# Seven quarter products for the source part of a four-layer adjacency aggregation

## Chip, cores, metric

One core of one Trainium2 chip. The time is the device time of one execution in microseconds (us), median of several runs; lower is better. All timed runs used here of one kernel agreed within 0.6%.

## The reference, cut to what matters

Sixteen independent batches, each with 1024 nodes of 128 features and a dense 1024x1024 adjacency, all fp32. Layer 0 aggregates once with the raw adjacency. Then come four message layers with 1, 1, 2 and 3 chunks of 128 input features, which use the adjacency with normed rows (source part) and with normed columns (destination part):

```python
def _layer(nodes, adj, ws, bs, wd, bd, wn, bn, wu, bu):
    src_agg = jnp.einsum('bjv,bij->biv', nodes @ ws + bs, _l2norm(adj, 2))
    dst_agg = jnp.einsum('bjv,bji->biv', nodes @ wd + bd, _l2norm(adj, 1))
    self_rep = nodes @ wn + bn
    return jnp.tanh(jnp.concatenate([src_agg, self_rep, dst_agg], axis=2) @ wu + bu)
# layers three and four concatenate features kept from earlier layers
x = _layernorm(x + _L0_gnn_ref(x, adj, adj, W, b))        # layer 0
x = _layernorm(x + _L1_gnn_ref(x, adj, ...))              # layers one to four
```

## The kernel before

The adjacency is held twice: as loaded with columns scaled (`a`, destination part) and transposed with rows scaled (`at`, source part). Messages are computed first (`messages`), then `aggregate` runs pairs of products of 64 columns side by side, one into partitions 64 to 127 (`high`) and one into 0 to 63 (`low`) of PSUM banks. The destination part is a 2x2 block product done by seven quarter products instead of eight (Strassen's scheme in Winograd's form), from sums of quarters `T2`, `T3`, `T4` of the adjacency and sums `S` of the messages. The source part is direct: eight blocks for each half of the nodes and each half of the features.

```python
upper = [                                    # into partitions 64..127
    (pz0, True, own(1, 0) + [src(1, 0, j) for j in range(4)], None),
    (alpha, True, dst(0, 0, quarter(a, 0, 0)), first_read),
    (pz0, False, [src(1, 0, j) for j in range(4, NB)], None),
    (alpha, True, mixed(2, T2), second_read),
    (pz0, False, dst(1, 1, T4), None),
    (alpha, True, mixed(3, T3), third_read),
    (pz1, True, own(1, 1) + [src(1, 1, j) for j in range(2, NB)], None),
]
lower = [                                    # into partitions 0..63
    (pz0, True, own(0, 0) + [src(0, 0, j) for j in range(NB)], None),
    (pz1, True, mixed(1, T1) + [src(1, 1, j) for j in range(2)], fourth_read),
    ...                                      # (cut)
]
for i, pair in enumerate(zip(up, lo)):
    if i in hooks:
        hooks[i]()        # work of other engines, and small products, ahead of pair i
    for o, x, y, start, stop, _ in pair:
        nc.tensor.matmul(o, x, y, start=start, stop=stop)
```

In the traces read here TensorE, VectorE and ScalarE run their instructions in the order of the program: in layer three `rp`, with key 5, comes behind 20 records of pairs (four a pair). So a key in `hooks` is a place in TensorE's order. While a batch runs its layers, the next batch's adjacency is loaded, its rows summed and squared (`sums`: ScalarE squares, GpSimd adds them up), its columns' sums of squares taken (`column_sums`, then a product `pc`), scaled, and its layer 0 is computed between layers three and four. Two small products: `rp` spreads the inverse norms of rows (layer three), `pv` sums squares for a layer norm (in layer four for the next batch, in layer one for the batch before).

```python
hooks = {0: factors, 5: factors_of_rows, 10: ...}              # layer three; rp is in factors_of_rows
hooks = {0: squares0, 5: rstd0, 11: end0, 15: rows0, ...}      # layer four; pv is in rstd0
hooks = {12: centre1, 18: rstd1, 27: end1}                     # layer one; pv is in rstd1
```

## Time and profile before

| | before |
|---|---|
| time, median | 2648.96 us |
| span in the profile | 2647.7 us |
| TensorE busy / not busy | 2592.4 / 55.3 us |
| mean granted TensorE clock (share of full speed) | 0.993 |

"Not busy" is the span less the busy time; it is the sum of all waits of TensorE, with start and end. Which waits those are is told by the view of waits (engine, tile, line, releaser: us in total, times, longest; PE is TensorE, PEld its loading of weights, DVE VectorE, ACT ScalarE, POOL GpSimd, SP SyncE, which issues transfers, and a q behind a name is that engine's queue):

```profile
PE pa L612 <- DMA raw<-in_L_gnn_wd_dram: 12.3, 1, 12.3
PE pv L325 <- DVE v L319: 7.6, 18, 2.2
...
PE rp L261 <- DVE sp L257: 2.4, 1, 2.4
```

A count of 1 is the start of the program. In the steady part only `pv` waits, some 0.25 to 0.4 us each time: TensorE is the bound.

### The profile page before, as it was taken

To read this page: it belongs to the slowest core of one execution; us is meant where nothing else is said; L and a number is where in the kernel's file an instruction comes from. 1 tells how busy PE (TensorE), PEld (TensorE's weight loads), DVE (VectorE), ACT (ScalarE), POOL (GpSimd) and SP (SyncE) were. 2 spreads that over 40 slices of the span, in tenths; PEclk is the share of its full clock that TensorE was granted. 3 is DMA by queue.
4 is the path that set the end of the run, shared out by engine and by line. 5 is a ranking of instruction groups with operands and counts; after the bars stand their busy time and mean duration, and the time that the engine had idled before them with its cause. 6 is when DMAs were issued, how large, how long until landed. Compare 5 with 4: busy or idle time off the path is not lost.

```text
span 2647.7 us, 29748 instructions
## 1 busy us (share of the span) xinstructions
PE 2592.4 (98%) x11313; PEld 1111.6 (42%) x11313; DVE 1517.7 (57%) x1978; ACT 731.2 (28%) x1374; POOL 505.5 (19%) x217
## 2 busy tenths in 40 slices
PE   5999999999999999999999999999999999999997
PEld 3444443433444344443444434334443444434443
DVE  5746656465564746557366564655647465574622
ACT  4413223141322413224132231413224132241311
POOL 5301203022030210303012030210302103030100
PEclk8999999999999999999999999999999999999998
DMA  7515214251241614315252142512315143152100
GB/s 163 107 49 113 48 57 92 58 125 45 71 77 51 125 45 102 64 53 105 58 114 48 57 92 58 126 45 75 73 50 126 45 104 63 55 103 58 50 9 8
DMA packets 358927, 196.44 MB, mean 74 GB/s; under 512 B 158800, under 2 KB 337872, under 8 KB 358784
## 3 DMA queue, kind: packets, MB, share of 16 engines
q1 hardware_dynamic: 355728, 190.27, 32.1%
q0 software_dynamic: 1648, 3.87, 0.7%
q8 instruction: 89, 1.46, 0.2%
q10 hardware_dynamic: 1408, 0.40, 0.1%
q14 instruction: 54, 0.44, 0.1%
HBM read 177.41 MB, written 17.02 MB: 73 GB/s over the span
## 4 chain that ended last, share of the span: by engine, by line
PE 94%; DVE 4%; DMA 1%; POOL 0%; SPq 0%; issue 0%; POOLq 0%; ACT 0%; ACTq 0%; DVEq 0%
PE p L527 67%; PE pt L423 15%; PE pa L350 8%; PE pw L361 1%; PE pw L362 1%; DVE v L319 1%; DVE y L310 1%; DMA raw<-in_L_gnn_bu_dram 1%; PE pv L325 0%; DVE t L427 0%; DVE at L386 0%; PE pm L309 0%; DVE t L436 0%; DVE S L437 0%; DMA raw<-in_L_gnn_wn_dram 0%
## 5 line engine op out<-in xcount | busy, mean ns | idle before, releaser
L527 PE MATMUL p<-at,t 128*64 128x512 f32 x3840 | 1133.7, 594 | 2.1 <-DVE at L386 2.1
L527 PE MATMUL p<-a,t 128*64 128x512 f32 x1536 | 687.1, 593 | 0.0
L527 PEld LDWEIGHTS p<-at,t 128*64 128x64 f32 x3840 | 356.6, 137 | 489.1 <-issue 477.9
L329 POOL TENSOR_TENSOR rs<-ve,mhalf 128x32 f32<-128x32 f32 (+1 forms) x34 | 174.4, 5130 | 1682.5 <-DVE ve L327 1682.5
L527 PE MATMUL p<-T,S 128*64 128x512 f32 x1024 | 463.5, 593 | 0.0
L427 DVE TENSOR_TENSOR t<-pt,bsd 128x512 f32<-128x512 f32 x256 | 173.9, 684 | 200.3 <-PE pt L423 200.3
L527 PEld LDWEIGHTS p<-a,t 128*64 128x64 f32 x1536 | 207.9, 137 | 147.3 <-issue 146.5
L527 PEld LDWEIGHTS p<-T,S 128*64 128x64 f32 x1024 | 139.0, 137 | 281.7 <-issue 279.6
L216 POOL TENSOR_TENSOR acc<-acc,sq 128x1024 f32<-128x1024 f32 x90 | 214.8, 2387 | 124.6 <-ACT sq L212 121.0
L527 PE MATMUL p<-T,t 128*64 128x512 f32 x512 | 233.4, 594 | 0.0
L527 PE MATMUL p<-a,S 128*64 128x512 f32 x512 | 233.2, 593 | 0.0
L381 ACT ACTIVATE st<-st,rinv 128x256 f32<-128x256 f32 x512 | 210.6, 494 | 14.5 <-DMA st<-in_adj_dram 12.0
L423 PE MATMUL pt<-wall,f1T 128*128 128x256 f32 x768 | 213.5, 383 | 0.0
L287 DVE TENSOR_TENSOR a<-a,cinv 128x1024 f32<-128x1024 f32 (+1 forms) x132 | 146.4, 1172 | 113.1 <-DMA cinv<-dr 105.2
L350 PE MATMUL pa<-a,xn 128*128 128x512 f32 x480 | 210.0, 595 | 0.0
L386 DVE STREAM_TRANSPOSE at<-st 128x512 f32<-128x512 f32 x256 | 162.0, 682 | 7.3 <-issue 7.3
L471 ACT COPY e<-p 64x512 f32<-64x512 f32 x64 | 37.2, 581 | 453.3 <-PE p L527 453.3
L423 PEld LDWEIGHTS pt<-wall,f1T 128*128 128x128 f32 x768 | 142.8, 190 | 44.7 <-issue 26.1
L527 PE MATMUL p<-f1T,wall 128*64 128x512 f32 x384 | 149.0, 601 | 0.0
L480 ACT COPY e<-e 64x512 f32<-64x512 f32 x64 | 39.3, 615 | 366.8 <-DVE e L479 366.8
L350 PEld LDWEIGHTS pa<-a,xn 128*128 128x128 f32 x480 | 90.0, 190 | 119.8 <-issue 119.8
L210 DVE TENSOR_REDUCE cols<-a 128x1 f32<-128x1024 f32 x120 | 139.0, 1208 | 0.5
(138 smaller groups left out, 2817.0 us busy)
## 6 DMA issues: line engine op xcount, KB each, us to landing
st<-in_adj_dram SPq DMA_DIRECT2D x1024, 64.0 KB, 2.0
a<-in_adj_dram SPq DMA_DIRECT2D x120, 512.0 KB, 12.8
xn<-in_x_dram SPq DMA_DIRECT2D x128, 64.0 KB, 1.9
kept<-y SPq DMA_DIRECT2D x16, 512.0 KB, 2.8
xk<-kept SPq DMA_DIRECT2D x16, 512.0 KB, 3.8
xs<-in_x_dram SPq DMA_DIRECT2D x60, 128.0 KB, 13.4
cinv<-dr SPq DMA_DIRECT2D x30, 256.0 KB, 6.3
dinv<-dr SPq DMA_DIRECT2D x30, 256.0 KB, 5.2
```

Source lines behind the costliest of these rows:

```text
L210: nc.vector.reduce_sum(cols[:, 2 * NB + i:2 * NB + i + 1], a[:, i, :], axis=AX.X)
L216: nc.gpsimd.tensor_add(acc, acc, sq)
L287: engine.tensor_mul(a[:, i, s], a[:, i, s], cinv[:, s])
L329: nc.gpsimd.tensor_tensor(rstd, ve, mhalf[:, :n], ALU.pow)
L350: nc.tensor.matmul(pa, xn[:, i], a[:, i, s], start=(i == 0), stop=(i == NB - 1))
L381: nc.scalar.activation(st[:, k], st[:, k], AF.Copy, scale=rinv[:, q * QB + k:q * QB + k + 1])
L386: nc.vector.transpose(at[h][:, j:j + NJ, o:o + QB * C].rearrange("p j (k c) -> p j k c", c=C), st.rearrange("p k (j c) -> p j k c", c=C)[: ...
L423: nc.tensor.matmul(pt[:, q], f[:, i * P:(i + 1) * P], w[:, c, 0:2].rearrange("p k v -> p (k v)"), start=(k == 0), stop=(k == nch - 1))
L427: nc.vector.tensor_add(t[j][:, o:o + 2], pt, bsd[l][:, None, :].to_broadcast([P, 2, 2 * P]))
L471: nc.scalar.copy(e0[high], alpha[high])
L480: nc.scalar.copy(e1[high], e0[high])
L527: nc.tensor.matmul(o, x, y, start=start, stop=stop)
```

## The change

The intent: use seven quarter products for the source part too, in layers two to four, and pay for the room it needs (three sums of quarters `Q2`, `Q3`, `Q4` of the transposed side) by staging rows in the old adjacency's place, fetching message weights again from memory for each layer, and sharing other buffers. The second half of the nodes is finished first. The heart of the diff, for layers two to four, with cuts:

```diff
-        upper = [ (pz0, True, own(1, 0) + [src(1, 0, j) ...]), (alpha, True, dst(...)), ... ]
+            upper = [
+                (Z1, True, own(1, 1)), (Z0, True, own(1, 0)),
+                (A, True, prod("M1", DST) + prod("M1", SRC)), (Bk, True, prod("M2", DST) + prod("M2", SRC)),
+                (A, True, prod("M3", SRC)),
+                (Z0, False, prod("Z21", SRC) + prod("Z21", DST)),
+            ]
+            lower = [
+                (Z1, True, own(0, 1)), (Z0, True, own(0, 0)),
+                (A, True, prod("M4", DST) + prod("M4", SRC)), (Bk, True, prod("M3", DST)),
+                (Z1, False, prod("Z12", SRC) + prod("Z12", DST)),
+                (Z0, False, prod("Z11", SRC) + prod("Z11", DST)),
+            ]
+            events = {8: first_reads, 12: lambda: nc.scalar.copy(e1[high], Bk[low]), 16: m2_and_half_of_m3,
+                      20: last_reads}
@@ sums
-            nc.vector.reduce_sum(cols[...], a[:, i, :], axis=AX.X)
+            if i < BPH:
+                nc.scalar.activation(sq, a[:, i, :], AF.Copy, accum_out=degree)
+            else:
+                nc.vector.reduce_sum(degree, a[:, i, :], axis=AX.X)
@@ layer one
-            hooks = {12: centre1, 18: rstd1, 27: end1}
+            hooks = {0: begin1, 10: centre1, 12: squares1, 14: rstd1, 20: end1}
@@ layer two
+            for i in ((3, 4) if b == 0 else (2, 3, 4)):
+                combine(i, yt, Q)                      # Q2, Q3, Q4 at step 0
+            for i in ALL:
+                hooks[1 + 3 * i] = lambda i=i: sums(n, a2, st, (i,))
+            hooks[26] = lambda: column_sums(n, st)
+        aggregate(b, 1, feats, t, a, at, T, Q, f23, "acc", hooks)
@@ layer three
-            hooks = {0: factors, 5: factors_of_rows, 10: lambda: scale(0), ...}
+            hooks = {1: factors, 11: lambda: scale(0, 1), ...}     # factors now holds rp too
@@ layer four
-            hooks = {0: squares0, 5: rstd0, 11: end0, 15: rows0, 19: rows1, 23: rows2, "half": rows3, 33: rows4}
+            hooks = {0: squares0, 3: rstd0, 10: rows0, 11: end0, 18: quarters0, 23: rows1, 26: rows2, 31: rows3}
```

Note for later that `Bk` is one bank with two users: the lower half takes `M3`, which ScalarE copies out at step 12 (counted without the own products), and the upper half takes `M2`, whose products go on from step 12.

## The prediction

> **What bounds the kernel now.** I read, in order, the page's busy times and slices, the chain of waits that ended last, the timeline of VectorE and TensorE at the starts of layers, and the groups by line.
>
> ```profile
> PE 2592.4 (98%) x11313; PEld 1111.6 (42%) x11313; DVE 1517.7 (57%) x1978; ACT 731.2 (28%) x1374; POOL 505.5 (19%) x217
> ...
> PE   5999999999999999999999999999999999999997
> ```
>
> TensorE is busy in all slices but the first and last; VectorE is busy little more than half of the time. Busy time alone does not prove a bound, so the chain is next (start us, length us, what), one piece of one batch:
>
> ```profile
> 1272.77 4.44 PE p L527 x20
> 1277.21 0.34 PE rp L261 x2
> 1277.55 25.04 PE p L527 x116
> 1302.60 13.93 PE pa L350 x32
> ...
> 1319.96 10.37 PE pt L423 x48
> 1330.33 0.02 issue
> 1330.36 0.69 DVE t L427
> 1331.05 1.13 DVE y L310
> ...
> 1333.96 1.14 DVE v L319
> 1335.10 0.04 issue
> 1335.15 0.41 PE pv L325 x2
> 1335.56 26.76 PE p L527 x124
> ```
>
> The chain lies on TensorE except for about 5 us at the start of layer four, where it runs over VectorE. There TensorE was still mostly working: its wait for pv was about 0.4 us. The unit to count in: one step of the aggregation is a pair of 64-column products, run beside each other, and leaves four records (two products, two passes each). So 116 records are 29 pairs in 25.04 us: 0.863 us a pair. A batch holds 134 pairs (115.7 us), the message stages (3.65, 3.65, 7.11 and 10.37 us in the chain, 24.8 together), 16 pa products (13.9), 4 pw (3.4) and six small products of about 0.34 us (2.0): 159.8 us. The same point of the next batch in the trace is 160.66 us later. So TensorE does nothing but work: each pair removed is worth 0.863 us, and each new wait of TensorE costs its full length.
>
> [...] So a small product that waits for VectorE holds everything behind it; the 0.4 us wait for pv above agrees. [...] 128x512 takes 0.69 us and 128x2048 2.29 us. Back to back they start 0.61 us apart for 128x512. [...] in layer two, beside the row sums on GpSimd (line L216), the small 128x256 combinations took 2.47 us instead of 0.42:
>
> ```profile
> 1239.34 2.47 DVE L436 TENSOR_TENSOR t<-t,t 128x256 f32<-128x256 f32 x1
> 1241.85 2.46 DVE L437 TENSOR_TENSOR S<-t 128x256 f32<-128x256 f32 x1
> 1244.23 0.28 DVE L439 TENSOR_TENSOR diff<-t 128x128 f32<-128x128 f32 x1
> ```
>
> **The change, part by part.**
>
> *Pairs.* Counting the two lists of the aggregation: 2n+30 pairs in each layer before (n = chunks of features). After: layer one still 2n+30, layers two to four 2n+28. Only two pairs fewer, because seven quarter products instead of eight save the source part one of eight, which is 4 of its 32 half-width products. That is 3 x 16 x 2 = 96 pairs, 96 x 0.863 = 83 us, all on the bound. This is the whole gain: an ideal 2566 us.
>
> *VectorE.* Four quarter sums of 128x2048 on the transposed side are added per batch: 4 x 2.29 = 9.2 us. Four row reductions of 1.21 us go to ScalarE (-4.8). The message combinations grow from 128x256 to 128x512 in layers two to four, about +1.2 us each. Some +8 us a batch; VectorE goes from 57% to some 62%. On average nothing, so what matters is where TensorE waits for it.
>
> *Order at the start of a layer.* Two things come together: the four combinations, which VectorE does in order ahead of everything else, take longer; and the small products that depend on later VectorE work are placed earlier in TensorE's order. I followed the order of instructions in the built changed kernel with durations from these lines:
>
> ```profile
> 1272.81 0.69 DVE L427 TENSOR_TENSOR t<-pt,bsd 128x512 f32<-128x512 f32 x1 [1.04 <-PE pt L423]
> 1273.42 0.42 DVE L435 TENSOR_TENSOR S<-t 128x256 f32<-128x256 f32 x1
> ...
> 1275.78 0.15 DVE L257 TENSOR_TENSOR sp<-inv,group 128x32 f32<-128x32 f32 x1
> ...
> 1277.14 0.41 PE L261 MATMUL rp<-sp,fold 128*128 128x32 f32 x2
> ```
>
> Layer three (messages end at 1272.7 here). Before, rp comes after five pairs and sp was done at 1275.9: no wait. After, rp comes after one pair, at 1273.6. VectorE: message add at 1272.8, combinations at +0.6, +1.3, +2.0, +2.7, the first factor instruction at +3.4, the end of sp 0.7 later: 1276.9. TensorE waits 3.3 us. 15 batches have a successor: 50 us.
>
> Layer four. pv comes after three pairs instead of five: pm ends at 1330.4, so TensorE is there at 1333.0. VectorE: add 1330.4, centring 1331.0, four combinations from 1332.1 with 0.6 to 0.7 us each, the reduction v (1.21 us) from 1334.8 to 1336.0. Wait 3.0 us, less the 0.4 of before: 2.6 x 15 = 39 us.
>
> Layer one (15 batches). The distance from pm to pv was six pairs and is four, 3.45 us. Between them VectorE now does a part of e0 (0.6), the centring (1.2), a quarter sum T4 (2.2) that has been put ahead of v, and v (1.2): 5.2 us. Wait about 1.4 us: 21 us.
>
> Layer two. The first quarter products need the sum of messages, right after two own pairs (1.7 us); VectorE needs about 2.0 us: 0.3 us x 16. At its end the column sums wait for GpSimd's last addition, which starts later than before because the next adjacency is loaded later; I get the second half of the features up to 1 us late: 0.6 x 15. Together 14 us.
>
> *Transfers.* Rows go straight from the old adjacency's place; before, 137 GB/s came at half the DMA engines' share. 1 MB should take 5 to 8 us and is then scaled and transposed some 20 us later: hidden. The next adjacency is loaded some 17 us later in layer one and takes 20 us at 206 GB/s; its first half lands just as ScalarE wants it. Refetched weights (at most 512 KB) are hidden by a whole layer.
>
> *Start and end.* Batch 0 multiplies columns before its first quarter product, where eight source pairs used to hide it: about +5 us. The first weights no longer fetch ahead of the adjacency: a few us either way. The tail stays the same.
>
> *Sum.* 2649 - 83 + 50 + 39 + 21 + 14 + 5 = 2695 us.
>
> **Rivals.** (A) The waits are hidden and the pairs count in full: 2566 to 2590 us, faster. For it: TensorE is the bound in every slice, and the change's intent. Against: the two long waits follow from in-order engines and durations that the trace shows, and before had just 0.4 us to spare at one of the very places. (B) The waits grow: GpSimd's additions hold the quarter sums in layer two (0.42 us became 2.47), or the idle of 3 us drops the granted clock. In the start of this trace an idle of about 3 us near 62 us was followed by a clock of 0.5 for some 3 us, one of 2 us near 88 us was not. One such drop costs at most 1.7 us; in every batch at two places 50 us. 2720 to 2750 us, slower. (C) A late transfer (rows or adjacency) holds ScalarE, which is in order, and then the features: 2 to 3 us a batch, 2725 to 2745.
>
> **Range and chances.** The mechanism puts the waits at 7 us a batch at least, against 5.2 saved, so about 2670 is the low side; hidden additions of (B) and (C) push up more often than down. Range 2655 to 2740. The border of slower is 2702, only 7 us above my number. Faster 0.05, within 2% 0.57, slower 0.38.
>
> **What would show it.** Right: some 384 aggregation records fewer on TensorE (96 pairs of four); a batch of about 163.5 us; waits of TensorE for sp (about 3 us, 15 times), for v in layer four (about 3) and in layer one (about 1.4), with the chain going over VectorE's combinations there. Wrong: a batch of 155 to 156 us with rp and pv not waiting (A); a clock clearly under 0.99, or VectorE additions of over 4 us beside GpSimd (B); waits for DMA on ScalarE or TensorE in the steady part (C).

The sum (2695 us): its durations are those of the trace of the kernel before (the 0.69 and 2.29 us are fp32 additions on VectorE). That the work behind a waiting product waits too, the runs show at `rp`: in the changed kernel the products behind it stood still for its 3.40 us, and where seven more pairs were put ahead of it they ran and the wait was gone (e2_rp). The 1.7 us of a drop of the clock are an estimate from the same trace: after the idle time near 62 us (3.00 us) the clock was 0.50 for some 3.4 us.

## The result

Ratios here are the mean time of one kernel's runs over that of the kernel before in the same rounds, so not quite the ratio of the medians quoted.

The changed kernel takes **2908.75 us** (4 runs, 2907.93 to 2911.35), ratio 1.0983 (95%: 1.0964 to 1.1002). It is 260 us slower; the prediction was 46 us slower. First the page of the changed kernel: the busy times, and the chain that ended last by engine ("issue" is time in which an engine waited for nothing that the profile shows).

```profile
PE 2611.0 (90%) x10929; PEld 1145.0 (39%) x10929; DVE 1674.3 (58%) x1974; ACT 830.0 (29%) x1549; POOL 511.9 (18%) x217
...
PE 64%; DVE 13%; DMA 8%; SPq 5%; ACT 4%; issue 4%; POOL 2%; POOLq 0%; DVEq 0%; ACTq 0%
```

The same line of the chain for the kernel before:

```profile
PE 94%; DVE 4%; DMA 1%; POOL 0%; SPq 0%; issue 0%; POOLq 0%; ACT 0%; ACTq 0%; DVEq 0%
```

TensorE has 384 records fewer, as intended, and only 64% of the chain lies on it (94% before). Yet its busy time *rose*, by 18.6 us, where the removed 96 pairs should have lowered it by 82.8. That contradiction is worth stopping at: fewer records that take longer in all must be slower records. The mean granted clock says the same: 0.966 against 0.993. So the difference of the two spans, 258.1 us, splits exactly:

- work removed: 96 x 0.863 = -82.8 us
- TensorE not busy: 294.8 (2905.8 - 2611.0) against 55.3: **+239.5 us**
- the rest of the busy time, 2611.0 - (2592.4 - 82.8) = **+101.4 us**. I call it stretch. Counted in slices of 3 us between 150 us and 60 us before the end, the changed kernel has 35 separate drops of the clock, 143 us at half speed in all, the kernel before none; so about 72 us of the stretch are seen directly there. Over the whole span the mean clock accounts for at most some 80 us of it (about 98 us of clock lost, 18 before); the other 20 or so are not explained.

The view of waits names the 239.5:

```profile
PE pv L347 <- DVE v L341: 73.4, 32, 3.0
PE p L581 <- ACT e L559: 69.8, 48, 3.6
PE rp L283 <- DVE sp L279: 51.5, 16, 3.4
PE pt L445 <- DVE t L448: 31.1, 15, 3.0
PE p L581 <- ACT e L502: 20.1, 16, 1.3
```

Three places show how these come about. **Layer three**, the chain of waits (start, length, what), just after the last message group:

```profile
1402.03 0.70 DVE S L458
...
1403.48 0.70 DVE S L460
...
1404.21 0.69 DVE S L461
...
1405.46 0.08 DVE sp L279
...
1405.68 0.60 PE rp L283 x2
```

VectorE works through four combinations before it comes to `sp`, and `rp` stands one pair behind the messages in TensorE's order: a wait of 3.4 us. Layer four has the same picture with `pv` behind v (3.0 us). Both are as predicted.

**Layer two** is what the prediction did not have. ScalarE's timeline, then TensorE's (start, length, engine, line, operation, shape; in brackets the idle time before and its releaser):

```profile
1374.31 1.06 ACT L231 ACTIVATE sq<-a 128x1024 f32<-128x1024 f32 x1
...
1375.49 1.06 ACT L234 ACTIVATE sq<-a 128x1024 f32<-128x1024 f32 x1
...
1376.55 1.04 ACT L234 ACTIVATE sq<-a 128x1024 f32<-128x1024 f32 x1
...
1377.70 0.58 ACT L559 COPY e<-p 64x512 f32<-64x512 f32 x1
```

```profile
1371.26 3.76 PE L581 MATMUL p<-T,S 128*64 128x512 f32 x15
1378.33 1.12 PE L581 MATMUL p<-Q,S 128*64 128x512 f32 x1 [3.32 <-ACT e L559]
...
1381.76 0.59 PE L581 MATMUL p<-Q,S 128*64 128x512 f32 x1
```

L559 is the copy of `Bk[low]`. The next product of `M2` goes to `Bk[high]`, other partitions of the same bank, and it waits for that copy. TensorE's last products end at 1375.0. The copy could run then, but ScalarE, in order, has one pass over 1024 columns under way and two more ahead of it, and runs it at 1377.70. The wait is in the program: the built code has, on the first product on `Q`, a wait for ScalarE. It could have been read before predicting; I took reads and writes of different partitions to be independent. The built program here waits for the whole bank (or for the tile, which fills the bank; the two can't be told apart here), at up to 3.6 us a time, though the copy reads partitions 0 to 63 and the products write 64 to 127. Whether they could run side by side here no run shows: taking the wait away alone was not tried.

**The clock.** The same lines show the second cost: the product after the wait takes 1.12 us, and 0.59 us three microseconds later. The windows view (window, length, busy us and count of each engine, then granted clock, DMA share, GB/s):

```profile
1379.00:1382.00 3.00, 3.00 (x10) 0.85 (x8) 0.00 (x0) 1.15 (x2) 2.84 (x3) 0.55 0.00 0
1382.00:1386.00 4.00, 4.00 (x20) 1.26 (x18) 1.54 (x3) 1.51 (x2) 2.00 (x1) 1.00 0.00 0
```

In the first window 0.55 is the clock: TensorE counts as busy for the whole 3 us and does little more than half the work. In the batch from 1343 to 1520 us this happens three times, after the waits of 3.32 (L559), 3.40 (rp) and 3.04 us (pv); not after those of 1.6 us and below. In these three the granted clock is 0.50 to 0.55 and a drop lasts some 3.4 us. The whole run is less regular. Laid beside the records of the clock, its 35 drops (28 of some 3.4 us, 7 of some 6.8) follow all 15 waits of `rp` (3.40 us), but only 8 of the 15 waits of `pv` in layer four (3.04 us), 10 of the 14 in layer two (2.88 to 3.58 us), and 2 waits of `pt` (1.74 and 2.73 us); none follows the 15 waits of `pv` in layer one (1.60 us). So the length of a wait alone does not decide whether a drop follows.

### The profile page after: what moved, and what is told of

The parts are those of the page before. It is cut to its first block, busy times and chain, and to the rows that moved or that the text cites. A ratio compares the mean times of both kernels' runs of the same rounds, so it can differ in the third digit from the quotient of the medians. Undisturbed runs are those within 1.5% of the kernel's fastest.

```text
span 2905.8 us, 28577 instructions
## 1 busy us (share of the span) xinstructions
PE 2611.0 (90%) x10929; PEld 1145.0 (39%) x10929; DVE 1674.3 (58%) x1974; ACT 830.0 (29%) x1549; POOL 511.9 (18%) x217
## 4 chain that ended last, share of the span: by engine, by line
PE 64%; DVE 13%; DMA 8%; SPq 5%; ACT 4%; issue 4%; POOL 2%; POOLq 0%; DVEq 0%; ACTq 0%
PE p L581 43%; PE pt L445 11%; PE pa L372 7%; DMA a<-in_adj_dram 5%; SPq L217 2%; POOL rs L351 2%; SPq L396 2%; DVE at L406 2%; DVE t L448 2%; DVE y L332 1%; DVE v L341 1%; ACT a L401 1%; DMA out_dram<-y 1%; PE pw L383 1%; PE pw L384 1%
## 5 line engine op out<-in xcount | busy, mean ns | idle before, releaser
L581 PE MATMUL p<-at,t 128*64 128x512 f32 x2112 | 583.4, 593 | 0.0
L581 PE MATMUL p<-a,t 128*64 128x512 f32 x1536 | 481.2, 602 | 6.1 <-DVE a L425 5.5
L581 PE MATMUL p<-Q,S 128*64 128x512 f32 x768 | 359.7, 624 | 69.8 <-ACT e L559 69.8
L581 PE MATMUL p<-T,S 128*64 128x512 f32 x1024 | 301.3, 594 | 20.1 <-ACT e L502 20.1
L581 PEld LDWEIGHTS p<-at,t 128*64 128x64 f32 x2112 | 195.9, 137 | 213.2 <-issue 192.7
L448 DVE TENSOR_TENSOR t<-pt,wm 128x512 f32<-128x512 f32 x256 | 173.0, 686 | 157.5 <-PE pt L445 156.8
L581 PE MATMUL p<-at,S 128*64 128x512 f32 x448 | 224.9, 646 | 0.0
L445 PE MATMUL pt<-wm,f1T 128*128 128x256 f32 x768 | 214.8, 385 | 0.0
L401 ACT ACTIVATE a<-a,rinv 128x256 f32<-128x256 f32 x480 | 197.3, 493 | 23.0 <-DMA a<-in_adj_dram 22.9
L581 PE MATMUL p<-Q,t 128*64 128x512 f32 x384 | 172.6, 592 | 0.0
```

The source lines that it names most:

```text
L401: nc.scalar.activation(st[:, k], st[:, k], AF.Copy, scale=rinv[:, q * QB + k:q * QB + k + 1])
L445: nc.tensor.matmul(pt[:, q], f[:, i * P:(i + 1) * P], wm[:, 1 + c], start=(k == 0), stop=(k == nch - 1))
L448: nc.vector.tensor_add(t[j][:, o:o + 2].rearrange("p k a v c -> p k (a v c)"), pt, wm[:, 0][:, None, :].to_broadcast([P, 2, 2 * P]))
```

## The experiments

All kernels gave the right result. Edits are on the changed kernel unless said otherwise. Idle is the span less TensorE's busy time; stretch is busy time above the work at full clock, as worked out above (2509.6 us, for e4 38.8 more, for e8 and before 2592.4, so that before has none by definition). Both are from one profiled run each; median and ratio from the timed runs.

| run | median us | ratio to before | clock | idle | stretch |
|---|---|---|---|---|---|
| before | 2649 | 1 | 0.993 | 55.3 | 0 |
| changed | 2908.75 | 1.0983 | 0.966 | 294.8 | 101.4 |
| e1_bank | 2947.76 | 1.1118 | 0.940 | 277.2 | 166.2 |
| e2_rp | 2830.16 | 1.0678 | 0.973 | 236.6 | 81.0 |
| e3_pv4 | 2828.27 | 1.0674 | 0.975 | 241.4 | 76.0 |
| e4_fill | 2887.73 | 1.0897 | 0.968 | 249.7 | 91.8 |
| e5_shift | 2734.41 | 1.0313 | 0.978 | 165.8 | 52.2 |
| e6_shift_bank | 2684.13 | 1.0124 | 0.981 | 122.6 | 48.3 |
| e7_quarters_early | 2678.52 | 1.0101 | 0.978 | 119.8 | 57.1 |
| e8_before_early | 2724.94 | 1.0276 | 0.989 | 116.4 | 13.9 |
| e9_place | 2659.41 | 1.0039 | 0.982 | 102.8 | 42.0 |
| e10_place_quarters | 2659.11 | 1.0032 | 0.983 | 101.5 | 41.6 |
| e11_reduce | 2620.36 | 0.9886 | 0.991 | 88.2 | 24.1 |
| e12_last_sum | 2590.21 | 0.9775 | 0.991 | 63.7 | 14.0 |

My theory: the removed pairs are worth what they should be, and placement loses more than that; each named wait is a separate cost, and waits of 3 us cost more than their length. The main rival: the waits stand for one another, because VectorE, ScalarE and GpSimd finish the same chain at the same time wherever TensorE waits for it; take one away and the next shows.

**e1_bank**: the copies out of the shared bank wait until both halves are done.

```diff
-            events = {4: m1_read, 6: lambda: m4_read(Bk), 8: m2_read, 12: m3_read, 18: second_half}
+            events = {4: m1_read, 8: m4_and_m2_read, 12: m3_read, 18: second_half}
@@ layers two to four
             def m2_and_half_of_m3():
+                nc.scalar.copy(e1[high], Bk[low])
                 m2_read()
-            events = {8: first_reads, 12: lambda: nc.scalar.copy(e1[high], Bk[low]), 16: ..., 20: last_reads}
+            events = {8: first_reads, 16: ..., 20: last_reads}
```

> The changed kernel with one thing moved: the ScalarE copies out of the lower half of the accumulator bank that M2 is still filling in its upper half are issued only after M2 is done (in layer one beside the second read, in layers two to four at step 16 instead of 12). Theory (same-bank wait): M2 or its second half waits for that copy, which in layer two stands behind the row sums in ScalarE's order; the waits for lines L559 and L502 (about 110 us of weight-load waits plus 34, some 6 to 7 us a batch with the copy itself) go, and with the 3.3 us one in layer two goes a drop of the clock (1.7 us). Expected 90 to 130 us off 2909: 2780 to 2820. Rival (VectorE is behind as a whole, so a wait removed comes back at the next small product): under 40 us off, above 2870, with longer waits for v and sp.

Measured: 39 us *slower* than the changed kernel, a plain miss. Waits of TensorE:

```profile
PE pv L347 <- DVE v L341: 90.4, 32, 3.0
PE rp L283 <- DVE sp L279: 52.0, 16, 3.4
PE pt L445 <- DVE t L448: 45.4, 15, 4.2
PE pc L264 <- DVE part L246: 40.9, 16, 5.0
```

The waits for L559 and L502 (89.9 us) are gone; pv grew by 17.0, pt by 14.3, and pc, which did not wait in the changed kernel after the start (5.0 us), has 40.9 with it. Idle fell by 17.6 us only, and stretch rose by 64.8. The trace shows why: the wait of pv in layer one went from 1.60 to 2.73 us, pt's from 1.59 to 2.92 or 3.68, and pc's from nothing to 2.39 us, and each of these was followed by a drop of the clock. In slices of 3 us there are 74 drops instead of 35. So the rival holds here, with an addition: breaking waits of 3.3 us into several of 2.4 to 3 us cost more clock here than it saved waiting.

**e2_rp** and **e3_pv4**: one small product each, later in TensorE's order.

```diff
-            hooks = {1: factors, 11: lambda: scale(0, 1), ...}
+            hooks = {1: factors, 8: factors_of_rows, 11: lambda: scale(0, 1), ...}   # e2: rp
-            hooks = {0: squares0, 3: rstd0, 10: rows0, ...}
+            hooks = {0: squares0, 8: rstd0, 10: rows0, ...}                            # e3: pv of layer four
```

> The changed kernel with only the product rp of layer three moved from behind pair 1 to behind pair 8. Theory of the prediction (the wait for sp costs its length): 3.4 us times 15 off, 51 us; with the clock drop that follows it (about 1.6 us, granted clock 0.5 for some 3.4 us) 75 us: 2830 to 2860. If the clock drop does not belong to this wait: 2855 to 2860. Rival (VectorE behind as a whole): under 20 us off.

> The changed kernel with only the product pv of layer four moved from behind pair 3 to behind pair 8. Theory: the wait of 3.0 us and the clock drop after it (1.6 us) go, 45 to 70 us off: 2840 to 2865. The norm then ends later on VectorE, some 4 us, which may give 0 to 15 us back through the transposes at the end of the layer. Rival: under 20 us off.

Measured: -79 and -80 us, a little more than expected for each. By the table e2 takes 58.2 us from idle and 20.4 from stretch, e3 53.4 and 25.4. In e2 the wait for sp is gone; in e3 pv's falls from 73.4 to 27.7, so layer four's share was 45.7 us, 3.0 a batch. These two waits are separate costs, and each microsecond of idle time that goes takes another 0.35 to 0.48 of stretch with it. In e2 that is a net figure: the 15 drops after rp are gone, while the waits of pv in layer four are now followed by a drop in all 15 batches instead of 8.

**e4_fill**: the first pair of layer three is computed three times more before rp, 45 useless pairs.

```diff
+            again = 3 if l == 2 and i == 0 and b + 1 < B else 0
-            for o, x, y, start, stop in pair:
+            for o, x, y, start, stop in [p[:4] + (True,) for p in pair] * again + list(pair):
```

> The changed kernel with useless work added: in layer three the first pair is computed three more times (2.6 us of TensorE, same result since each starts afresh) just ahead of rp, where TensorE waits 3.4 us for sp. Theory [...]: the clock stays at 1 after rp, so although TensorE does 45 pairs more the kernel gets faster, by about 1.6 us times 15, 15 to 25 us: 2884 to 2894, and the mean granted clock rises from 0.966 to about 0.975. Rival (the clock drop comes from something else, or its cost is not on the path): the time stays within 5 us of 2909 or gets longer.

Measured: -21 us, with 38.8 us more work. This is within the expectation, but not all of it for the expected reason: the wait for sp fell by 37.7 us, which the work replaces; pt's wait fell by 7.3, and stretch by only 9.6. Counted over the whole trace, the 15 drops after rp are gone, but pv's waits in layer four are followed by 15 drops instead of 8, and the time at half speed falls only from 143 to 137 us. Doing useless work cost nothing here against waiting; that the clock by itself is worth 15 to 25 us at this place is not shown.

**e5_shift**: rp and pv of layer four as in e2 and e3, pv of layer one from step 14 to 18 with its end later, and the scaling of one chunk of rows in layer four from 26 to 24.

```diff
-            hooks = {0: begin1, 10: centre1, 12: squares1, 14: rstd1, 20: end1}
+            hooks = {0: begin1, 10: centre1, 12: squares1, 14: rows1_1, 18: rstd1, 20: combine1, 26: end1}
-            hooks = {0: squares0, 3: rstd0, ..., 23: rows1, 26: rows2, 31: rows3}
+            hooks = {0: squares0, 8: rstd0, ..., 23: rows1, 24: rows2_scale, 26: rows2, 31: rows3}
```

> The changed kernel with the small products moved back behind work that does not wait: rp of layer three behind pair 8, pv of layer four behind pair 8, pv of layer one behind pair 18 (the row transposes stay at 14), and the scaling of row chunk 3 on ScalarE two steps earlier in layer four. The waits for the bank copies (L559, L502) stay. If the waits add up: 79 us (e2) plus 81 us (e3) plus about 3 us times 15 for layer one plus 1.6 times 15 for the late message sums: 2909 - 79 - 81 - 45 - 24, about 2680. If they come back elsewhere, as they did in e1: 2720 to 2800. Moving only makes the changed kernel as fast as before (2649) at best, since the bank waits stay.

Measured: 2734.41, in the range for waits that come back elsewhere. All waits of rp, pv and pt are gone from the steady part. What is left:

```profile
PE p L581 <- ACT e L559: 92.2, 48, 5.6
PE p L581 <- ACT e L502: 20.1, 16, 1.3
```

L559 grew from 69.8 to 92.2: again a part of what was removed came back at the next place. Pv of layer one and the chunk of rows were moved together, so neither is measured by itself.

**e6_shift_bank** puts e1's edit on e5.

> The one before, and also the bank copies moved behind both halves (as in e1). Theory from e1 (layer two is bound by another chain: ScalarE squares, GpSimd additions, column sums, pc): the waits for L559 and L502 go, but in layer two a wait for the column sums of about 2.4 us and a clock drop remain; about 2 us a batch off against the one before at most: 2640 to 2680. If the bank waits were what bounds layer two: 6 us a batch off, 2580 to 2600.

Measured: 2684.13, 50 us below e5, more than the 2 us a batch expected at most, and just above the expected range. The same edit that cost 39 us alone gains 50 here, which fits that fewer other waits stand ready. In the place of the 112 us for L559 and L502 stand pc (41.0) and the messages of layer three, which wait 31.4 us for the features of layer two.

**e7_quarters_early**: on e6, the sums Q2 and Q3 move from the start of layer two to the end of layer one, to unload VectorE where the chain now lies.

```diff
-            hooks = {..., 20: combine1, 26: end1}
+            hooks = {..., 20: combine1, 22: lambda: quarters1(2), 24: lambda: quarters1(3), 27: end1}
-            for i in ((3, 4) if b == 0 else (2, 3, 4)):
+            for i in ((3, 4) if b == 0 else (4,)):
```

> The one before, and two of the three quarter sums of the transposed side moved from the start of layer two to the end of layer one, where VectorE is idle for 5 us and GpSimd runs nothing. Theory (in layer two the quarter sums and GpSimd's additions hold each other up: Q3 took 4.34 us instead of 2.29): the additions end some 3 to 5 us earlier, the wait for the column sums goes, and with it its clock drop: 30 to 60 us off against the one before, 2580 to 2630, faster than the kernel before. Rival (the chain is bound by ScalarE's copies and squares alone, or by the late load): under 10 us off.

Measured: 2678.52, a miss: VectorE's sums were not what the chain waited for. (The profiled run, 2688.34, is the slowest of its four, so its row in the table is on the high side.) The trace showed another thing: in layer two ScalarE stands 2.21 us waiting for the store of the batch before (its buffer holds layer two's partial sums next), which is still behind the next adjacency's load.

**e8_before_early**: the kernel *before*, with nothing changed but the places of rp and pv (layers three and four), as the change has them.

```diff
-            hooks = {0: factors, 5: factors_of_rows, ...}
+            hooks = {0: factors, 1: factors_of_rows, ...}
-            hooks = {0: squares0, 5: rstd0, ...}
+            hooks = {0: squares0, 3: rstd0, ...}
```

> The kernel before (no change) with only the two places moved as the change moved them: rp of layer three behind pair 1 instead of 5, pv of layer four behind pair 3 instead of 5. Theory (the placing alone costs its waits): rp waits about 2.4 us and pv 1.7 us more than now, 15 times: 62 us; without clock drops 2710, with a drop after each (1.6 us) 2760. Rival (the waits are there only because the message combinations grew): within 10 us of 2649.

Measured: 2724.94, +74 us against the kernel before in the same rounds (2650.67), between the two expected numbers. So moving two products of 0.34 us a few pairs ahead costs the good kernel 61 us of idle time and 14 of stretch, without any of the other parts of the change. The waits are 2.2 us for rp and 2.0 us for pv in all 15 batches; 7 drops of the clock follow, all of them after rp.

**e9_place** and **e10_place_quarters**: e6 and e7 with layer two's partial sums in another buffer, so that they need not wait for the store. For that the spread inputs, whose place they take, are fetched later.

```diff
-        aggregate(b, 1, feats, t, a, at, T, Q, f23, "acc", hooks)
+            hooks[24] = lambda: st.update(xs=load_spread(n))
+        aggregate(b, 1, feats, t, a, at, T, Q, f23, "x", hooks)
```

> e6 (small products and bank copies moved), and layer two's partial sums put in the place of the spread inputs, which are fetched after them, instead of the place of the outputs of the batch before, whose store stands behind the 4 MB load. Theory (in layer two ScalarE waits some 5 us for that store with the row sums behind it, so the additions, the column sums and the second half of the features come late): the waits for pc and for the features in layer two (41 and 31 us) shrink to under a third and the clock drops with them: 60 to 90 us off against e6, 2595 to 2625, faster than the kernel before. Rival (ScalarE's copies and GpSimd's additions are too long by themselves): under 15 us off.

> e7 (as e6, and two quarter sums early), with the same new place for layer two's partial sums. If both the store and the collision of quarter sums with GpSimd's additions hold layer two up: another 10 to 25 us off against e9, 2575 to 2605; the ideal is 2649 - 83 + 5, about 2570. If only the store does: within 8 us of e9.

Measured: 2659.41 and 2659.11. The wait for layer two's features fell from 31.4 to 5.5 us; pc's stayed (45.9 and 45.4). ScalarE's wait for the store (2.21 us in the batch read in e7) is gone in the same place in e10, and the time fell by 25 us from e6 to e9; that the later fetch of the spread inputs has no part in this was not tested by itself. So the store was a cost, and Q2 and Q3 make no difference even now. The gain is smaller than expected since pc, with 2.8 us a batch, remained; that its wait would shrink too did not come true. Its chain in e9:

```profile
947.36 2.35 POOL acc L238
...
949.74 1.26 DVE acct L244
951.01 0.04 DVE part L246
```

pc waits for GpSimd's last addition of squares. The chain goes on back through ScalarE's last square, the tanh and copies ahead of it, VectorE's additions between them, and GpSimd's earlier additions, to ScalarE's first passes over the rows and the load of the adjacency: ScalarE makes two passes over each of the first four rows since the change.

**e11_reduce**: on e10, these four row reductions back to VectorE.

```diff
-            if i < BPH:
-                nc.scalar.activation(sq, a[:, i, :], AF.Copy, accum_out=degree)
-            else:
-                nc.vector.reduce_sum(degree, a[:, i, :], axis=AX.X)
+            nc.vector.reduce_sum(degree, a[:, i, :], axis=AX.X)
```

> e10, with one part of the change undone: the four row reductions of the next adjacency that ScalarE did as copies with an accumulator go back to VectorE, which is idle for some 7 us in layer two once two quarter sums are done early. Theory (what bounds layer two now is the chain ScalarE copies and squares, GpSimd's additions, column sums, pc; the copies put 2.5 us ahead of the first addition and hold the square's place in the buffer): the chain ends 4 to 6 us earlier, the wait for pc (2.7 us a batch) goes and so does the clock drop after it (1.6 us): 50 to 65 us off against 2659, 2595 to 2610, some 2% faster than the kernel before. Rival (GpSimd's additions collide with the reductions on VectorE or with the load, so the chain ends as late as now): within 10 us of 2659.

Measured: 2620.36, -39 us; the direction as expected, the size some 10 us short. pc waits 20.1 us instead of 45.4. In exchange TensorE waits 12.6 us for VectorE's combinations at the start of layer two, one or two of which took 2.7 to 2.9 us instead of 0.70 beside GpSimd.

**e12_last_sum**: on e11, the last row's sum two steps earlier.

```diff
-                hooks[1 + 3 * i] = lambda i=i: sums(n, a2, st, (i,))
+                hooks[min(1 + 3 * i, 20)] = lambda i=i: sums(n, a2, st, (i,))
```

> e11, with the square and addition of the last row of the next adjacency issued two steps earlier in layer two (step 20 instead of 22), ahead of the second-half copies in ScalarE's order. Theory (what is left of the wait for pc, 20 us in all, comes from GpSimd standing idle for some 3 us before its last addition because the square waits behind those copies): 10 to 20 us off, 2600 to 2612. Rival (the square must wait for GpSimd to free its buffer anyway, and then holds the copies up): within 5 us of 2620, or longer.

Measured: **2590.21 us** (5 runs, 2582.85 to 2591.01), ratio 0.9775 (0.9762 to 0.9789), better than expected: faster than both kernels. Its chain of waits over the same part of a batch, layer three's start included, lies on TensorE alone, and pc and rp are passed without a wait:

```profile
1396.43 3.65 PE pt L442 x16
1400.08 0.14 PE pc L261 x2
1400.22 3.54 PE pt L442 x16
1403.76 7.02 PE p L582 x32
1410.78 0.34 PE rp L280 x2
```

Against e11 idle fell by 24.5 us and stretch by 10.1. Idle is 63.7 us (before: 55.3) and stretch 14.0. 63.7 - 55.3 + 14.0 - 82.8 = -60.4 us, which is the difference of the two spans: nearly three quarters of the removed work show in the time once the waits are gone.

## Why the prediction was wrong, step by step

- **Pairs, -83 us: right.** 384 records fewer; with e12's waits gone, 60 of the 83 us show in the time.
- **Layer three, +50: right.** rp waits 3.4 us (predicted 3.3), 51.5 in all.
- **Layer four, +39 net of before's wait: right.** 3.0 us (predicted 3.0), 45.7 in all by the difference of e3. Layer one, predicted 1.4 us: 1.6 us in each batch. (Its own terms give 5.2 - 3.45 = 1.75 us; the 1.4 was a slip that cost nothing.)
- **Layer two, +14: failed.** "The first quarter products need the sum of messages ... 0.3 us": they did not wait for it. The wait there is for the copy out of the shared bank, 3.3 us in layer two and 0.7 in layers three and four, 1.3 in layer one (L502): 89.9 us, absent from the sum. The step had looked at VectorE and data only, not at who else uses the bank. But this term can't just be added to make the account right: e1 shows that without these waits others take their place.
- **Column sums, "up to 1 us late": right in kind, hidden in the result.** In the changed kernel pc shows no steady wait because TensorE already waited earlier in the layer; where that is taken away, pc waits 2.4 to 2.8 us (e1, e9). It was undersized because ScalarE's second pass over four rows was counted as relief for VectorE, not as length of the chain: undoing it gave 39 us (e11).
- **The scaling of the last rows in layer four: missing.** The messages of layer one wait 31.1 us in all, 1.6 us in seven batches and 1.7 to 3.0 in the others, for VectorE, which stood 3.98 us behind ScalarE's scaling (a chunk of rows placed after the tanh of the half). In e5 the wait is gone, where that scaling is two steps earlier; other things were moved too.
- **The clock, left out of the sum and put at 50 us at most in rival (B): failed in size.** The stretch is 101 us, of which some 72 are seen as half speed in the steady part. It was counted at two places of a batch, where 23 drops followed 30 waits; a third place was the unpredicted wait, with 10 more. Both signs that the prediction had named for (B) are there: the clock, and an addition of 4.34 us on VectorE beside GpSimd (`Q3` in layer two). Of these only the clock is seen to cost: moving `Q2` and `Q3` away gained 5.6 us on e6 and 0.3 on e9 (e7, e10).
- **Start, +5:** by the list of waits the start has lost the 12.3 us for weights and has 4.5 for the adjacency, 5.5 and 2.5 for scaled columns: about even; not tested by itself.
- **Transfers hidden: right for the weights, wrong for rows.** Refetched weights land in 2.9 to 3.5 us and never stop TensorE. For rows ScalarE waits 22.9 us in 12 waits, the sign named for rival (C): in the 8 batches where it waits 1.6 us or more, the messages of layer one wait longer than 1.6 us, 7.3 us more in all (in e3 none waits longer than 1.6 us). The store of the previous batch, which I had not followed, does delay ScalarE (2.21 us in e7's batch; e9, without it, is 25 us faster than e6).

The range failed for one reason above the others: it allowed for two predicted waits to be somewhat longer, not for a further set of waits as large as they are, nor for each long wait to cost about 1.4 times its length (e2, e3). Set side by side, the waits predicted at 50, 39 and 21 us came out at about 50, 40 and 24; the 14 for layer two stands against 90 for the bank, and 31 for late messages and 101 of stretch were not in the sum. That makes about 2902 of the measured 2909; it is an account of where TensorE waited, not of what each wait would give back if removed.

## What to carry to other kernels

A small product in TensorE's order belongs behind the last instruction of the engine that feeds it, counted in that engine's own order; two such products placed a few pairs early cost a tuned kernel about 75 us. Before trusting a saving on the bound, list what every product waits for in the built program, buffers and banks included, not only data. And when one wait is taken away and nothing is gained, look at what the next place waits for: the saving is there only when the whole chain of the other engines has been made shorter or moved.
